# A macaron block on one core: the planner of the issue order also tries 180 random shifts of urgency

## The chip, the cores and the metric

The kernel runs on one core of one Trainium2 chip. The metric is the device time in microseconds (us) of one execution, as the median of some runs. The engines are PE (TensorE, matmuls and transpositions), DVE (VectorE), ACT (ScalarE), POOL (GpSimd) and SP (SyncE, which here only issues DMAs). Each engine works through its own list of instructions in order; an instruction that waits for a semaphore holds up all that stand behind it on that engine.

## The reference

The input is 8 sequences of 1024 tokens with 256 features, in float32. Three residual parts follow each other:

```python
x = x + 0.5 * ffn(layernorm(x))
x = x + mamba(layernorm(x))
x = x + 0.5 * ffn(layernorm(x))
```

- `ffn`: gate and up matrices of 704 x 256, `silu(gate) * up`, and a down matrix of 256 x 704. Ahead of each of the three matmuls the activations, and once the weights, are rounded in blocks of 16 values to a grid of eight magnitudes (FP4) and scaled back.
- `mamba`: a normalisation, a projection to 2 x 512 channels x and z, a causal convolution of four taps over x and `silu`, a projection to a step size `delta` (softplus) and to B and C of 16 states, and the selective scan

```python
h = exp(delta * A) * h + delta * B * u     # over time, for 512 channels x 16 states
y = sum over the states of h * C  +  u * D
```

then `y * silu(z)` and a projection back to 256 features.

## The kernel before, in words

The tokens are cut into 16 chunks of 512, two to a sequence (`SPLIT`). For every chunk there are generators for the first feed-forward part (`stage_f1`), what precedes the scan (`stage_m1`), the z branch (`stage_z`), the scan (`scan`), and the output projection with the second feed-forward part (`stage_out`). The list `work` at the end of `macaron` interleaves them: the first feed-forward part of a chunk is emitted some chunks ahead of its scan and the second one behind it. So at any time the scan of one chunk shares the engines with feed-forward work of others.

The scan of a chunk runs over 16 states, k. For each state (`scan_step`): ACT scales the transposed `delta * u` by B (s_bu, L793, four tiles); then for each of four groups of 128 channels ACT computes the decay (s_da, L797), PE transposes s_bu into a PSUM bank (s_pb, L800, four transpositions; two banks, "psb", take turns), and DVE runs the recurrence over 512 steps (s_h, L802). If the sequence goes on, ACT keeps the last column (s_carry, L828). POOL multiplies the four groups by C, two at a time (`times_c`, L810), and then issues a DMA that adds the product to a sum in DRAM (accd, L835; the second state of a chunk stores plainly through SP instead). Four buffers hold s_h.

The feed-forward part of 128 tokens: PE makes half of gate (f_pg) and of up (f_pu, both L559), ACT takes a tanh (L562), DVE multiplies twice (L563, L564) into f_h. The rounding (`quant`) is a chain over three engines: DVE takes the blocks' maxima (q_mx, L459), POOL the scale (q_sc, L460), DVE its reciprocal (q_rc, L461), POOL multiplies (L462), ACT squares into PSUM (q_q, L466), DVE makes two passes that round (L467, L468), POOL multiplies by the scale (L469). The same chain runs over the normalised input, f_xn. Then PE transposes f_h (f_pa, f_pb), ACT copies (f_ht, L572, L576), PE multiplies by the down matrix (f_po, L579), and DVE adds to the residual x4 (L580).

The order of issue is not that of emission. When all is emitted, `set_order` (L338) builds a `Graph` of all instructions: `price` gives each one a cost by engine, kind and size; `LAG` what a semaphore between two engines takes (105 ns from POOL to POOL); buffers that are used again are edges as well. `Graph.plan` lays out a schedule on this model: it takes the engine that can start first and, of its instructions that are ready, the one with the smallest `prio`, with a little look-ahead (`LOOK`, `WAIT`). It models POOL and DVE holding a shared port, PE's start from cold, and one server for all DMAs. Run with `back=True`, it lays out the schedule from the end.

`set_order` makes a first plan from the order of emission and the longest path behind each instruction (L342), and then `PASSES` = 7 rounds: a plan from the end gives each instruction its latest start, and these starts are the priorities of the next plan from the front (L343 to L345). Of the eight plans, the one with the least total is taken (L347), and its order on each engine is written into the program as dependencies without semaphores. The instructions themselves, their buffers and their semaphores follow from the emitted program and from this order.

Of the kernel before, what the change touches and what calls it, by code (L numbers as in the profile page):

```python
# [3 lines left out]

# [75 lines left out]

WEIGHT = 0.2
LOOK = 600
WAIT = 30
PASSES = 7
TICK = 10240 / 3
PORT = 200
SLACK = 20000
# [82 lines left out]
class Graph:  # L172
# [85 lines left out]
    def plan(self, prio, back=False):  # L258
# [18 lines left out]
        while len(order) < self.n:  # L277
# [40 lines left out]
            if not back and e == ET.PE:  # L318
                if passed[t // TICK - 1] < WARM:
                    more = hold  # L320
                passed[(t + hold + more) // TICK] += cols
                free[e] += more
# [15 lines left out]
def set_order(tc, tags, nbuf):  # L338
    insts = [i for i in tc.nc.cur_bb.bb.instructions if type(i).__name__ != "BassTilePoolBoundary"]
    g = Graph(insts, tags, nbuf)  # L340
    path = g.paths()
    found = [g.plan([x - WEIGHT * path[x] for x in range(g.n)])]  # L342
    for _ in range(PASSES):  # L343
        total, _, start = g.plan([-s - c[0] for s, c in zip(found[-1][2], g.cost)], back=True)
        found.append(g.plan([total - s - c[0] for s, c in zip(start, g.cost)]))  # L345
    prev = {}
    for x in min(found, key=lambda f: f[0])[1]:  # L347
        e = g.eng[x]
        if e in prev:
            tc.add_manual_dep(insts[x], insts[prev[e]].name, mybir.DependencyInfo(  # L350
                mybir.DependencyClass.NoSync, mybir.DependencyReason.DATA), reason="issue order")
        prev[e] = x
# [3 lines left out]
def macaron(ctx: ExitStack, tc: tile.TileContext, x_in, norm_w, norm_b, in_w, conv_w,  # L356
# [505 lines left out]
    for _, _, gen, kind[0] in sorted(work, key=lambda w: w[:2]):  # L862
        next(gen, None)
    set_order(tc, tags, nbuf)


# [26 lines left out]
```

## Time and profile before

| what | value |
|---|---|
| median of three runs | 2534.21 us (2523.82 to 2535.66) |
| the profiled execution: time | 2536.37 us |
| the profiled execution: span from first to last instruction | 2534.4 us |
| PE busy | 2344.9 us (93%), 10980 matmuls |
| DVE busy | 2184.4 us (86%), 3082 instructions |
| ACT busy | 2146.9 us (85%), 3952 instructions |
| POOL busy | 2177.2 us (86%), 1556 instructions |
| mean granted clock of PE | 0.985 |
| products h * C on POOL (L810) | 512, 1281.8 us, mean 2596 ns |
| accumulating DMAs from POOL (L835) | 238, 1024 KB each, 9.7 us to landing |

The profile is of one execution. Busy times are unions of the instructions' spans; an engine's idle time is what is left of the span. A float32 matmul or transposition is one instruction in the program; the profile can show a matmul as two. A wait names the instruction that stood still, and the one whose semaphore came last. The chain of waits goes back from the last instruction to what released each piece of it. A "product" below is an L810, a "scan step" an L802.

### The profile page before, as it was taken

How to read it: one execution, taken by the hardware profiler on the slowest of the kernel's cores; microseconds unless marked ns; L12 is line 12 of the kernel's file. 1: busy time of each engine (PE TensorE's matmuls, PEld its weight loads, DVE VectorE, ACT ScalarE, POOL GpSimd, SP SyncE). 2: the span in 40 equal slices, each digit the busy share in tenths (PEclk: the TensorE clock that was granted, in tenths of full speed). 3: DMA queues.
4: the chain of work that ended last, by engine and by line, in shares of the span. 5: the costliest groups of instructions: out<-in, count | busy, mean ns of one | idle time of the engine just before them, and what ended most of it. 6: DMA issues, size and time to landing. Idle time of an engine off the chain costs nothing.

```text
span 2534.4 us, 33625 instructions
## 1 busy us (share of the span) xinstructions
PE 2344.9 (93%) x10980; PEld 1591.6 (63%) x10980; DVE 2184.4 (86%) x3082; ACT 2146.9 (85%) x3952; POOL 2177.2 (86%) x1556
## 2 busy tenths in 40 slices
PE   5989898999999999999999999999999999888876
PEld 3555565766666666666666666666666666655544
DVE  7568797998989899898989899898989989878885
ACT  4489787998989988999888989898989988999842
POOL 4359798899989999899998999899997999899952
PEclk9989999999999999999999999999999999999998
DMA  3049779699888988789897998889896988999950
GB/s 90 9 117 207 194 163 223 163 186 238 166 197 195 218 202 189 205 171 239 176 219 173 201 221 176 211 173 221 195 202 181 189 225 175 216 235 211 232 127 17
DMA packets 113647, 465.57 MB, mean 184 GB/s; under 512 B 14592, under 2 KB 32896, under 8 KB 76864
## 3 DMA queue, kind: packets, MB, share of 16 engines
q0 software_dynamic: 36576, 266.35, 56.3%
q1 hardware_dynamic: 76896, 197.08, 24.2%
q8 instruction: 86, 1.41, 0.2%
q14 instruction: 89, 0.73, 0.1%
HBM read 146.19 MB, written 317.19 MB: 183 GB/s over the span
## 4 chain that ended last, share of the span: by engine, by line
POOL 36%; PE 27%; issue 11%; DVE 9%; ACT 9%; DMA 8%; POOLq 0%; SPq 0%; DVEq 0%; ACTq 0%
POOL s_h L810 20%; PE f_pg L559 4%; PE f_pu L559 4%; PE f_po L579 4%; PE s_pb L800 4%; POOL accd L835 4%; DVE s_h L802 4%; DMA accd<-s_h 3%; PE m_pc L682 3%; POOL f_h L462 3%; POOL f_h L469 3%; ACT s_bu L793 2%; ACT s_da L797 2%; POOL f_xn L469 2%; POOL o_y L771 2%
## 5 line engine op out<-in xcount | busy, mean ns | idle before, releaser
L810 POOL TENSOR_TENSOR s_h<-s_h,s_cbc 128x1024 f32<-128x1024 f32 x512 | 1281.8, 2596 | 51.7 <-ACT s_carry L828 27.0
L797 ACT ACTIVATE s_da<-m_delta,an 128x512 f32<-128x512 f32 x1024 | 714.5, 715 | 44.5 <-DVE s_h L802 42.8
L793 ACT ACTIVATE s_bu<-m_duT,m_bc 128x512 f32<-128x512 f32 x1024 | 693.4, 715 | 15.6 <-PE s_pb L800 14.1
L800 PEld LDWEIGHTS s_pb<-ident,s_bu 128*128 128x128 f32 x4096 | 498.0, 142 | 330.2 <-issue 123.4
L800 PE MATMUL s_pb<-ident,s_bu 128*128 128x128 f32 x4096 | 639.2, 277 | 50.9 <-DVE s_h L802 47.4
L802 DVE TENSOR_TENSOR_SCAN s_h<-s_da,s_carry,s_pb 128x512 f32<-128x512 f32 x512 | 636.5, 1265 | 16.5 <-PE s_pb L800 13.3
L802 DVE TENSOR_TENSOR_SCAN s_h<-s_da,s_pb 128x512 f32<-128x512 f32 x512 | 604.4, 1206 | 35.0 <-PE s_pb L800 21.1
L579 PE MATMUL f_po<-wdn,f_ht 128*128 128x256 f32 x1536 | 393.1, 387 | 11.5 <-ACT f_ht L576 6.8
L559 PE MATMUL f_pg<-wg,f_xt 128*128 128x352 f32 x1024 | 370.5, 473 | 13.7 <-ACT f_xt L549 6.2
L559 PE MATMUL f_pu<-wu,f_xt 128*128 128x352 f32 x1024 | 365.6, 468 | 14.1 <-DVE f_h L563 8.4
L579 PEld LDWEIGHTS f_po<-wdn,f_ht 128*128 128x128 f32 x1536 | 276.1, 192 | 73.3 <-ACT f_ht L576 17.0
L835 POOL DMA_DIRECT2D accd<-s_h x238 | 230.7, 969 | 31.8 <-POOL s_h L810 24.1
L559 PEld LDWEIGHTS f_pu<-wu,f_xt 128*128 128x128 f32 x1024 | 182.6, 193 | 115.7 <-issue 34.5
L682 PE MATMUL m_pc<-m_xp,cdg 128*128 128x512 f32 x512 | 252.7, 595 | 2.4 <-ACT m_car L679 2.4
L469 POOL TENSOR_TENSOR f_h<-f_h,q_sc 128x704 f32<-128x704 f32 x128 | 206.5, 1616 | 54.9 <-DVE f_h L468 50.5
L559 PEld LDWEIGHTS f_pg<-wg,f_xt 128*128 128x128 f32 x1024 | 180.3, 195 | 93.4 <-issue 15.1
L462 POOL TENSOR_TENSOR f_h<-f_h,q_rc 128x704 f32<-128x704 f32 x120 | 184.9, 1541 | 22.7 <-DVE q_rc L461 21.9
L563 DVE SCALAR_TENSOR_TENSOR f_h<-f_h,f_pg 128x352 f32<-128x352 f32 x256 | 128.7, 506 | 86.4 <-ACT f_h L562 85.5
L460 POOL TENSOR_SCALAR q_sc<-q_mx 128x44 f32<-128x44 f32 (+2 forms) x198 | 98.0, 497 | 88.5 <-DVE q_mx L459 83.8
L564 DVE TENSOR_TENSOR f_h<-f_h,f_pu 128x352 f32<-128x352 f32 x256 | 129.5, 507 | 41.6 <-PE f_pu L559 39.9
L562 ACT ACTIVATE f_h<-f_pg 128x352 f32<-128x352 f32 x256 | 115.6, 456 | 48.1 <-PE f_pg L559 46.6
L776 PE MATMUL o_po<-outw,o_y 128*128 128x256 f32 x512 | 129.3, 387 | 5.5 <-POOL o_y L771 2.9
(110 smaller groups left out, 3299.6 us busy)
## 6 DMA issues: line engine op xcount, KB each, us to landing
accd<-s_h POOLq DMA_DIRECT2D x238, 1024.0 KB, 9.7
s_cbc<-cd SPq DMA_DIRECT2D x128, 512.0 KB, 5.6
accd<-m_ud SPq DMA_DIRECT2D x64, 256.0 KB, 9.3
accd<-s_h SPq DMA_DIRECT2D x16, 1024.0 KB, 6.8
szd<-m_tz SPq DMA_DIRECT2D x64, 256.0 KB, 6.8
o_y<-accd SPq DMA_DIRECT2D x16, 1024.0 KB, 9.9
o_y<-accd POOLq DMA_DIRECT2D x16, 1024.0 KB, 9.1
o_sz<-szd SPq DMA_DIRECT2D x30, 512.0 KB, 5.1
```

What stands on the lines that cost most here:

```text
L462: mul0.tensor_tensor(vb, vb, rc.unsqueeze(2).to_broadcast([P, g, BLK]), ALU.mult)
L469: mul1.tensor_tensor(vb, vb, sc.unsqueeze(2).to_broadcast([P, g, BLK]), ALU.mult)
L559: nc.tensor.matmul(dst, xt[:, c, :], w[:, c, hf * FH : (hf + 1) * FH], start=(c == 0), stop=(c == 1))
L564: nc.vector.tensor_tensor(hh, hh, pu, ALU.mult)
L579: nc.tensor.matmul(po, ht[:, k, :], wdn[:, k, :], start=(k == 0), stop=(k == NF - 1))
L682: nc.tensor.matmul(pc, cdg[:, dc, k, :], xp[:, k : k + n], start=(k == 0), stop=(k == KC - 1))
L793: nc.scalar.activation(b, duT[s][t], AF.Copy, scale=bcol[s][:, t, k : k + 1])
L797: nc.scalar.activation(da, delta[s][dc], AF.Exp, scale=an[:, dc, k : k + 1])
L800: nc.tensor.transpose(pb[:, t * P : (t + 1) * P], bu[t][:, dc * P : (dc + 1) * P], ident)
L802: nc.vector.tensor_tensor_scan(h[:, dc, :], da, pb, init, ALU.mult, ALU.add)
L810: eng_c.tensor_tensor(hv, hv, cbc.unsqueeze(1).to_broadcast([P, cm, n]), ALU.mult)
L835: nc.gpsimd.dma_start(accd[s][j, :, :, :n], h, accum_op=ALU.add)
```

## The change

In `set_order` the loop of passes keeps the best plan of those that the seven passes made and its priorities (`prio`) rather than a list. The first plan of all counts only until the first pass. Then the instructions are grouped by the kind of tile that they write (its name without the number) and by engine; groups of fewer than 16 are left out. With a generator of fixed seed, 180 trials follow. Each takes one to three groups, draws for each a shift from a normal distribution with a spread of 1, 4 or 12 us, adds it to the priorities of all instructions of that group, and plans anew. A trial whose total is below the best is kept, and the next trial starts from its priorities. The order of the best plan is written into the program as before. All that stands behind it is as it was, 25 lines further down.

```diff
+import random
...
+TRIALS = 180
+SHIFT = (1e3, 4e3, 12e3)
...
-    found = [g.plan([x - WEIGHT * path[x] for x in range(g.n)])]
+    best = last = g.plan([x - WEIGHT * path[x] for x in range(g.n)])
+    prio = None
     for _ in range(PASSES):
-        total, _, start = g.plan([-s - c[0] for s, c in zip(found[-1][2], g.cost)], back=True)
-        found.append(g.plan([total - s - c[0] for s, c in zip(start, g.cost)]))
+        total, _, start = g.plan([-s - c[0] for s, c in zip(last[2], g.cost)], back=True)
+        late = [total - s - c[0] for s, c in zip(start, g.cost)]
+        last = g.plan(late)
+        if prio is None or last[0] < best[0]:
+            best, prio = last, late
+    groups = defaultdict(list)
+    for x, i in enumerate(insts):
+        for a in i.outs:
+            if hasattr(a, "bass_ap"):
+                groups[a.bass_ap.tensor.name.rsplit("_", 1)[0], g.eng[x]].append(x)
+    groups = [u for u in groups.values() if len(u) >= 16]
+    rng = random.Random(4)
+    for _ in range(TRIALS):
+        late = list(prio)
+        for u in rng.sample(groups, rng.choice((1, 2, 3))):
+            d = rng.gauss(0.0, rng.choice(SHIFT))
+            for x in u:
+                late[x] += d
+        f = g.plan(late)
+        if f[0] < best[0]:
+            best, prio = f, late
     prev = {}
-    for x in min(found, key=lambda f: f[0])[1]:
+    for x in best[1]:
```

## The prediction

> **What bounds the kernel now.** I read the stretches first: busy time from the start to the first scan step (157 us), from there to the last scan step (2443 us), and behind it. Columns: sum of the stretch, then busy us (and instructions) of PE, its weight loads, DVE, ACT and POOL, the granted clock, DMA share and GB/s.
>
> ```profile
> 0.00:157.00 157.00, 123.15 (x437) 77.30 (x438) 93.26 (x171) 79.17 (x166) 58.05 (x79) 0.96 0.20 61
> 157.00:2443.00 2286.00, 2157.97 (x10304) 1471.44 (x10301) 2037.34 (x2823) 2048.05 (x3746) 2099.38 (x1455) 0.99 0.88 198
> 2443.00:2534.00 91.00, 63.77 (x242) 42.83 (x242) 53.76 (x89) 19.71 (x41) 19.82 (x23) 0.90 0.11 31
> ```
>
> The middle is nine tenths of the time. No engine is full in it: PE is idle for 128 us of 2286, POOL for 187, ACT for 238, DVE for 249. Four engines at 89 to 94% that hand short pieces to each other: the end is set by who waits for whom. The chain that ended last says the same; no engine has half of it:
>
> ```profile
> POOL 36%; PE 27%; issue 11%; DVE 9%; ACT 9%; DMA 8%; POOLq 0%; SPq 0%; DVEq 0%; ACTq 0%
> ```
>
> Then the waits of the middle stretch: engine and line, what it waited for, total us, times, longest. The longest three each of POOL, ACT and DVE, and the one of PE that matters:
>
> ```profile
> DVE f_h L563 <- ACT f_h L562: 63.7, 52, 7.4
> PE s_pb L800 <- DVE s_h L802: 47.4, 77, 2.5
> ACT s_da L797 <- DVE s_h L802: 42.8, 69, 1.9
> DVE s_h L802 <- PE s_pb L800: 34.4, 57, 2.6
> DVE q_rc L461 <- POOL q_sc L460: 33.3, 31, 5.0
> ...
> POOL q_sc L460 <- DVE q_mx L459: 28.9, 20, 8.9
> ...
> ACT q_q L466 <- POOL f_h L462: 27.8, 36, 2.4
> POOL s_h L810 <- ACT s_carry L828: 27.0, 18, 5.0
> ...
> POOL accd L835 <- POOL s_h L810: 24.1, 80, 0.4
> ...
> ACT m_delta L709 <- PE m_pd L708: 18.2, 11, 3.4
> ```
>
> The reader is to see many small waits, none of which is a bottleneck by itself. Leaving out waits for DMA and an engine's waits for itself, the named waits between engines add up to 128.7 us on POOL, 219.7 on DVE and 180.9 on ACT in this stretch.
>
> **What the change does to the order.** The same instructions are issued; only their order on each engine differs. I set the built order of the changed kernel against that of before, instruction by instruction. The first 125 instructions of ACT are the same, the first scan step stands at place 285 on PE in both and at 174 and 175 on DVE; behind the last product of the scan POOL has 27.6 and 23.8 us of work left, DVE behind the last scan step 52.0 and 50.5. So **start and end get nothing**: PE is the busiest engine in both, and the 4 us on POOL lie beside its matmuls. In the middle much moves, but not far: of the neighbouring pairs PE keeps 72%, POOL 40%, ACT 38%, DVE 32%; a scan step moves back by 1.4 places on DVE, the quantising passes over f_h and f_xn (L467, L468) forward by 1.3 and 1.8. The feed-forward part became a little more urgent, the scan a little less.
>
> **The terms.** A wait inside a round trip can be counted from an order: A on engine X releases B on Y, B releases C on X. The work between A and C on X, at the mean durations of the trace, is the cover; if it is short, C waits. I sorted the round trips of before by cover, took the mean idle time ahead of C in each class from the trace, and counted the classes again in the new order.
>
> 1. PE's scan banks. Two PSUM banks take the transposed s_pb, so the block after next (L800) needs the scan step (L802) done. Of 1022 trips, cover under 0.65 us: 35 before, 29 after, at 0.56 us of PE idle each; 0.65 to 1.35: 77 and 58 at 0.24; 1.35 to 2: 318 and 334 at 0.03; over 2: 592 and 601 at nearly nothing. 6 x 0.56 + 19 x 0.24 - 16 x 0.03 = **7.4 us less**, of 50.4 in all: 15%.
> 2. The quantising trips on DVE (L459 to L461 by POOL, L461 to L467 by POOL and ACT), f_h and f_xn. Mean cover falls, 5.23 to 4.54 and 6.19 to 5.68 us for the second trip. By classes: -0.7 and +2.9 for f_h, +2.6 and +7.7 for f_xn, **12.5 us more** on DVE. The same trips as POOL sees them (L460 to L462, L462 to L469): +2.9, +1.0, +1.4, -2.1, **3.2 us more**.
> 3. POOL's accumulating DMA (L835). Where it stands right behind the product whose result it sends, POOL idles 0.33 us ahead of it; behind anything else, 0.03 us (82 and 156 in before). The new order has 116 of the first kind: 34 x 0.29 = **9.9 us more** on POOL. Behind it in POOL's queue stand the next products and quantising steps, and the scan waits for them.
> 4. PE changes its kind of work 3196 times and not 2984. A transposition starts 144 ns ahead of a following f_po matmul and 131 ns ahead of its own kind: 13 ns x 212 = 2.8 us more on PE, if nothing hides it.
> 5. The products on POOL (L810) fall into classes: 152 of 512 last under 2.45 us, 282 last 2.45 to 2.76, 78 more. Which DVE work lies beside each is redrawn. If a twentieth, 26, change class either way, that is 26 x 0.27 = 7 us less or more; I take nothing.
> 6. All other waits between engines can't be counted from one engine's order, and these are what the trials aim at. Bounds: nothing, and the 128 us that PE is idle in the middle, the smallest idle sum. I take the share of term 1, 15% (0.147 unrounded), the only one with a count: it is a wait of the same kind and size as the others. That is my choice, and the weakest step.
>
> On term 5 the Trainium skill speaks against this change: "SBUF — State Buffer", section "SBUF: two separate sides", says that DVE and GpSimd take their shared port pair as an exclusive lock for a whole instruction, whichever starts first, and the other fully blocks. The two classes of the product's duration in this trace agree with that, but show no blocker by name. By the rule the duration of a product hangs on a few hundred ns of phase, which no plan made beforehand can hold over 2286 us; the plan's gain at that port would then be lost, and the sum would stand at its upper part. The sum here doesn't use it.
>
> **The sum.** Busy time in the middle does not change, so each engine's account is its idle time. POOL: -0.147 x 128.7 + 9.9 + 3.2 = -5.8. DVE: -0.147 x 219.7 + 12.5 = -19.8. ACT: -0.147 x 180.9 = -26.6. They must end at one figure; I take their mean, **-17.4 us** (PE's busy time has modelled ends, so its account is a rival below). The profiled execution took 2536.37 us, span 2534.4, 0.1% above the median of 2534.21 of the three runs, so nothing is converted: 2536.4 - 17.4 = **2519 us**, 0.6% below the median.
>
> **Rivals.** (a) PE's account is right: only terms 1 and 4 reach the end, -7.4 + 2.8 = -4.6, **2532 us**. For: PE has least idle time, and the chain is on it for 27%. Against: its waits in the profile are short, and POOL has more of the chain. (b) Slower: POOL's DMA issue. The waits that the trials take away come back at other places (shorter covers in term 2 point there), and what stays is POOL's line with products and issues back to back: from the end of a product to the start of what follows its DMA take 1.04 us when the issue stands directly behind it, 0.62 otherwise; 34 x 0.42 = 14.3 us more, **2551 us**. It decides once term 6 gives POOL less than 13 us. For: POOL has 36% of the chain, and the wait is on POOL itself, where no better timing elsewhere helps. Against: the wait is known to the planner, though at less than its measured size (0.105 us in its table). (c) The gain is twice my share: POOL -24.7, DVE -52.1, ACT -53.2, mean -43, **2493 us**. (d) That the trials keep nothing is excluded: the order differs.
>
> **Chances.** Forecast 0.42, (c) 0.06, (a) 0.32, (b) 0.20. About 0.5%, 13 us, is what a measurement of this kernel tells from no change: faster by more is the forecast and (c), 0.48; within it (a), 0.32; slower (b), 0.20. The forecast lies near the border, which is why (a) has so much. The range goes from (c) to (b), 2493 to 2551, and takes in the 7 us of term 5.
>
> **What would show it.** Busy sums equal within a per cent on DVE and ACT. Right: PE's wait for L802 in the middle down from 47.4 to about 40; the sums between engines down by a tenth or more on ACT and DVE; POOL's wait of L835 for L810 up from 24.1 to about 34 with some 114 occurrences; first scan step at 157 us and 91 us behind the last one, as now. Wrong: POOL's busy time over the products moved by more than 10 us (term 5), a new wait for DMA landings (the slots of s_h return sooner or later), or a start or end that moved by more than 5 us.

## The result, and the profile after

| | median us | runs | ratio, 95% |
|---|---|---|---|
| before | 2533.2 | 2523.82 to 2535.66 (4) | 1 |
| after | 2555.07 | 2552.52 to 2556.48 (4) | 1.0083, 1.0061 to 1.0105 |

The changed kernel is slower by 0.8%, where 0.6% faster was forecast; the time lies above the range. The profiled execution took 2554.48 us, with a span of 2552.7, 18.3 us more than before. Line numbers are now those of the changed kernel, 25 higher. First the stretches, cut in the same way (start, from the first scan step to the last, behind it), with the same columns:

```profile
0.00:155.00 155.00, 121.35 (x447) 75.72 (x448) 95.79 (x174) 80.44 (x169) 58.58 (x81) 0.98 0.21 64
155.00:2469.00 2314.00, 2170.71 (x10303) 1472.92 (x10301) 2040.74 (x2827) 2045.31 (x3745) 2103.16 (x1455) 0.98 0.87 196
2469.00:2553.00 84.00, 60.52 (x234) 42.10 (x234) 49.28 (x83) 19.09 (x39) 17.71 (x21) 0.89 0.07 22
```

The busy sums of DVE, ACT and POOL in the middle are those of before within 4 us; PE's is 13 us larger, at a granted clock of 0.98 and not 0.99. Measured exactly from the first scan step to the last, the middle grew from 2288.0 to 2314.2 us, and start and end gave back 4 us each. For DVE, ACT and POOL that is 24 to 28 us more of idle time, for PE 14. The waits of the middle (engine and line, what it waited for, total us, times, longest), the largest without PE's weight loads, and those that moved:

```profile
ACT s_da L822 <- DVE s_h L827: 60.8, 79, 2.2
PE s_pb L825 <- DVE s_h L827: 53.3, 82, 2.7
DVE f_h L588 <- ACT f_h L587: 50.2, 41, 7.1
DVE q_rc L486 <- POOL q_sc L485: 43.8, 44, 5.4
POOL accd L860 <- POOL s_h L835: 35.1, 116, 1.0
...
ACT m_duT L754 <- PE m_dt L752: 33.3, 21, 6.8
...
DVE bn_st L548 <- DMA x4c<-x1d: 21.9, 6, 5.7
DVE f_h L492 <- ACT q_q L491: 20.4, 27, 2.0
...
ACT m_tz L768 <- DMA accd<-m_ud: 14.5, 3, 8.0
```

The chain of waits is spread as before (POOL 33%, PE 27%, DVE 11%) and names no culprit. In the waits two lines for DMAs are of a new size. The load of x4c (L667) fetches the residual ahead of the Mamba part of a chunk; DVE waits 21.9 us for it in 6 places, against 4.5 in 4 before. ACT waits 14.5 us for a buffer that the store of m_ud (L745) reads, against 3.3.

Summed anew over every group of both traces, from the first scan step to the last, us before and after:

| waits of | for other engines | for DMAs | for itself |
|---|---|---|---|
| PE | 123.3, 137.5 | 0, 0 | 0, 0 |
| POOL | 131.8, 133.2 | 14.1, 20.1 | 27.2, 38.8 |
| DVE | 230.9, 236.9 | 4.9, 22.3 | 0, 0 |
| ACT | 210.3, 235.6 | 17.3, 23.5 | 0.2, 0 |

On DVE 17 of the 24 us more are for DMAs. On POOL the waits for other engines stayed as they were, and its own issue and the DMAs added to them. On ACT the growth is for other engines: for the scan step (s_da, 42.8 to 60.8) and for PE's transpositions (m_duT, 16.6 to 33.3). So in no engine did the waits for others fall.

What such a place looks like, at a border between two chunks near 1000 us; first the two stretches in the columns of above:

```profile
985.00:1000.00 15.00, 15.00 (x74) 10.16 (x73) 12.71 (x14) 13.13 (x21) 14.40 (x10) 1.00 1.01 253
1000.00:1015.00 15.00, 8.07 (x20) 4.10 (x19) 6.09 (x15) 6.44 (x10) 8.44 (x6) 0.70 1.03 257
```

Then what SP issued there in the kernel after (start, duration, line, transfer), and two of the instructions that stood waiting, on DVE and on PE; the bracket has the idle time ahead of an instruction and what ended it:

```profile
986.24 0.32 SPq L656 DMA_DIRECT2D x1d<-x4a  x1
988.50 0.32 SPq L745 DMA_DIRECT2D accd<-m_ud  x1
988.92 0.94 SPq L844 DMA_DIRECT2D s_cbc<-cd  x1
992.73 0.32 SPq L667 DMA_DIRECT2D x4c<-x1d  x1
```

```profile
1004.72 0.75 DVE L548 BATCH_NORM_STATS2 bn_st<-x4c 128x6 f32<-128x256 f32 x2 [3.77 <-DMA x4c<-x1d]
```

```profile
1006.41 2.71 PE L584 MATMUL f_pu<-wu,f_xt 128*128 128x352 f32 x4 [3.65 <-DVE f_h L588]
```

The reader is to see that the DMA share (the column ahead of GB/s) is 1.0 for 30 us: all 16 DMA engines are full. The load of x4c, issued at 992.73, lands 12 us later. DVE stands, then PE for 3.65 us, and the granted clock of that stretch is 0.70. The same border before: three stretches, SP's issues, and DVE's first read of x4c:

```profile
985.00:1000.00 15.00, 15.00 (x80) 10.88 (x78) 14.84 (x20) 13.65 (x24) 14.65 (x11) 1.00 1.01 203
1000.00:1015.00 15.00, 15.00 (x73) 10.22 (x72) 13.12 (x15) 11.53 (x20) 14.70 (x10) 1.00 1.03 258
1015.00:1030.00 15.00, 14.49 (x63) 9.04 (x62) 10.93 (x20) 13.85 (x23) 12.28 (x11) 1.00 1.00 292
```

```profile
1006.46 0.32 SPq L631 DMA_DIRECT2D x1d<-x4a  x1
1007.52 0.58 SPq L720 DMA_DIRECT2D accd<-m_ud  x1
1014.72 0.32 SPq L642 DMA_DIRECT2D x4c<-x1d  x1
1015.79 0.32 SPq L819 DMA_DIRECT2D s_cbc<-cd  x1
```

```profile
1025.33 0.43 DVE L523 BATCH_NORM_STATS2 bn_st<-x4c 128x6 f32<-128x256 f32 x1 [0.72 <-DMA x4c<-x1d]
```

Before, too, the DMA share is 1.0, for 45 us, and the load, issued at 1014.72, takes 10.6 us. But DVE has other work until then: it waits 0.72 us for x4c and not 3.77, and PE hardly pauses. Over all 15 loads the time from issue to landing is much the same in both kernels, 8.5 us in the median before and 8.7 after (the longest 12.2 and 13.6), while DVE's wait for them is five times as long. So full DMA engines and slow landings are no news of the order after. At this border it has less other work at hand until the load lands.

The lists of SP differ as well. At this border the broadcast of C (s_cbc) is issued ahead of the load after, and behind it before. Between a chunk's store of x1d and its load of x4c it stands at 9 of the 15 borders after, and at 4 before.

The two traces also differ in their course. After is 17 us ahead where chunk 4 (of 16) begins its scan, 725.7 against 742.8 us, and 19 us behind at chunk 13, 2079.8 against 2061.1.

### The profile page after: what moved, and what is told of

Same layout as the page of the kernel before. It is cut to its first block, busy times and chain, and to the rows that moved or that the text cites. A ratio compares the mean times of both kernels' runs of the same rounds, so it can differ in the third digit from the quotient of the medians.

```text
span 2552.7 us, 33598 instructions
## 1 busy us (share of the span) xinstructions
PE 2352.6 (92%) x10980; PEld 1590.8 (62%) x10980; DVE 2185.8 (86%) x3082; ACT 2144.8 (84%) x3952; POOL 2179.5 (85%) x1556
## 3 DMA queue, kind: packets, MB, share of 16 engines
q0 software_dynamic: 36576, 266.35, 56.1%
q1 hardware_dynamic: 76896, 197.08, 24.4%
## 4 chain that ended last, share of the span: by engine, by line
POOL 33%; PE 27%; DVE 11%; issue 10%; ACT 10%; DMA 8%; POOLq 0%; SPq 0%; DVEq 0%; ACTq 0%
POOL s_h L835 18%; DVE s_h L827 6%; PE f_pg L584 5%; PE f_po L604 4%; PE f_pu L584 4%; PE s_pb L825 4%; POOL accd L860 3%; ACT s_da L822 3%; POOL f_h L487 3%; ACT s_bu L818 3%; POOL f_h L494 2%; DMA accd<-m_ud 2%; PE m_pc L707 2%; DMA x4c<-x1d 2%; PE o_po L801 1%
## 5 line engine op out<-in xcount | busy, mean ns | idle before, releaser
L835 POOL TENSOR_TENSOR s_h<-s_h,s_cbc 128x1024 f32<-128x1024 f32 x512 | 1288.7, 2593 | 50.1 <-ACT s_carry L853 34.9
L822 ACT ACTIVATE s_da<-m_delta,an 128x512 f32<-128x512 f32 x1024 | 717.0, 716 | 63.8 <-DVE s_h L827 60.8
L825 PE MATMUL s_pb<-ident,s_bu 128*128 128x128 f32 x4096 | 646.4, 278 | 56.1 <-DVE s_h L827 53.3
L604 PE MATMUL f_po<-wdn,f_ht 128*128 128x256 f32 x1536 | 401.3, 385 | 7.1 <-ACT f_ht L597 3.3
L584 PE MATMUL f_pu<-wu,f_xt 128*128 128x352 f32 x1024 | 376.8, 476 | 23.3 <-DVE f_h L588 19.3
L584 PE MATMUL f_pg<-wg,f_xt 128*128 128x352 f32 x1024 | 375.7, 476 | 16.5 <-DVE f_h L588 9.8
L604 PEld LDWEIGHTS f_po<-wdn,f_ht 128*128 128x128 f32 x1536 | 270.4, 192 | 71.6 <-issue 16.8
L860 POOL DMA_DIRECT2D accd<-s_h x238 | 223.4, 939 | 47.5 <-POOL s_h L835 35.1
L494 POOL TENSOR_TENSOR f_h<-f_h,q_sc 128x704 f32<-128x704 f32 x128 | 200.4, 1570 | 68.7 <-DVE f_h L493 66.7
L487 POOL TENSOR_TENSOR f_h<-f_h,q_rc 128x704 f32<-128x704 f32 x120 | 184.4, 1538 | 25.1 <-DVE q_rc L486 22.5
L491 ACT ACTIVATE q_q<-f_h 128x704 f32<-128x704 f32 x128 | 97.1, 759 | 49.6 <-POOL f_h L487 36.1
```

The costliest lines, as they stand in the source:

```text
L487: mul0.tensor_tensor(vb, vb, rc.unsqueeze(2).to_broadcast([P, g, BLK]), ALU.mult)
L494: mul1.tensor_tensor(vb, vb, sc.unsqueeze(2).to_broadcast([P, g, BLK]), ALU.mult)
L584: nc.tensor.matmul(dst, xt[:, c, :], w[:, c, hf * FH : (hf + 1) * FH], start=(c == 0), stop=(c == 1))
L604: nc.tensor.matmul(po, ht[:, k, :], wdn[:, k, :], start=(k == 0), stop=(k == NF - 1))
L822: nc.scalar.activation(da, delta[s][dc], AF.Exp, scale=an[:, dc, k : k + 1])
L825: nc.tensor.transpose(pb[:, t * P : (t + 1) * P], bu[t][:, dc * P : (dc + 1) * P], ident)
```

## The experiments

Four theories stood against each other at first: late landings and the buffers they hold, of x4c and m_ud, cost the time (A); POOL's DMA issue behind its own product, rival (b) of the prediction, does (B); the many short waits of engines on each other do, whatever the DMAs do (C); the model's error is larger than its gain, so that a plan's rank says nothing of the chip (D). Formed on the way: the load of the DMA engines eats the gain (F); the order's early part is good and its later part bad (G); the order of SP's list, s_cbc ahead of x4c, does it (H). Every kernel was compared with its own runs of the kernel before, whose medians were 2531.4 to 2536.5 us. An "a" at the front of a name is the order after, a "b" the order before; the others have orders of their own.

### The landings: other sources and more buffers

a_x4c loads the residual from the input instead of from the store ahead of it; the planner is told the old dependency, so that the order stays. b_both and a_both have that and t2k (m_tz's and m_ud's buffers) with one buffer more.

```diff
-            nc.sync.dma_start(x4[:, :nt], x1d[s][:, :nt])
+            nc.sync.dma_start(x4[:, :nt], tok(x_in, s))
```

> The order of the changed kernel, instruction for instruction; only x4c (L642 in the numbering of before) is loaded from the input instead of from x1d, so that the load no longer waits for the store of x1d to land. The planner is still told of the old dependency, so the plan and all orders are the same. Left out: the first feed-forward part does not reach what the scan part reads. Theory A (landings: the new order puts users of DMAs earlier than they land; DVE stands still for x4c for 21.9 us in the changed kernel against 4.5 before): this wait falls under 5 us and the time by 12 to 20 us, to 2535 to 2543. Theory B (POOL's accumulating DMA issues stand right behind their products, 116 times against 82): nothing of it is touched, time within 5 us of 2555. Theory C (the scan step was made less urgent by 4 us, so ACT and PE wait for it): within 5 us of 2555.

Measured: 1.0128 (1.0111 to 1.0145), slower still. The wait for x4c went from 21.9 to 30.4 us: the load now stood waiting for its buffer, which an x1d store still had to read. It is also another load: from the input the same bytes come in four times the packets (82656 against 76896 on SP's queue, 384 more for each of the 15 loads).

a_t2k has only the fourth t2k buffer; for the room, the second half of the input projection's z weights is left out (the first half is read in its place):

```diff
-            xc = sb.tile([P, T], F32, tag="t2k", bufs=BUFS["t2k"], name="m_xc")[:, :n]
+            xc = sb.tile([P, T], F32, tag="t2k", bufs=BUFS["t2k"] + 1, name="m_xc")[:, :n]
```

> The order of the changed kernel, instruction for instruction; the tiles of the tag t2k (m_xc, m_ud, m_tz) get four buffers instead of three, so that m_tz need not wait until the DMA of an earlier m_ud has been read out (14.5 us of ACT's waits in the changed kernel, 3.3 before, and 15.3 against 3.5 us of DVE's for m_tz itself). To make room the second half of the z weights is left out (its matmuls read the first half's weights); the planner counts as before. Theory A (landings): these two waits fall under 5 us each and the time by 6 to 12 us, to 2543 to 2549. Theories B (POOL's DMA issues) and C (late scan steps): within 4 us of 2555.

> Both edits on the order of the changed kernel: x4c from the input, four buffers for t2k (left out: the first feed-forward part for the scan part, half of the z weights). Theory A (landings): waits for DMAs fall from 31 us on DVE and 26 on ACT to under 12 each; the time goes to 2525 to 2538, level with the kernel before. Theory B: 2555 less 5 at most, since its 11 us on POOL stay. Theory C: 2548 or more, since the waits for the scan step stay at 60.8 us on ACT and 53.3 on PE.

> The same two edits on the order of the kernel before (same parts left out). It shows how much these waits cost there: its waits for DMAs are 15 us on DVE and 20 on ACT. Theory A: 3 to 8 us less than 2533, so 2525 to 2530, and with both edits the two orders lie within 10 us of each other. Theories B and C: the distance of 20 us between the two orders remains with both edits.

Measured: a_t2k 1.004 (1.0026 to 1.0055), with ACT's wait for m_ud at 0; a_both 1.0078 (1.0049 to 1.0106); b_both 1.0001 (0.9984 to 1.0018). So the missing buffer is worth about 11 us to the order after. What it is worth to the order before isn't shown: b_both holds the other source too, which by itself cost the order after some 11 us.

a_x4t gives x4 and t2k a buffer more each; a_all and b_all add the other source.

```diff
-        x4 = sb.tile([P, NT, DM], F32, tag="x4", bufs=BUFS["x4"], name="x4a")
+        x4 = sb.tile([P, NT, DM], F32, tag="x4", bufs=BUFS["x4"] + 1, name="x4a")
```

> The order of the changed kernel, instruction for instruction, with four x4 buffers instead of three and four t2k buffers instead of three; the planner still counts three of each. To make room, in_proj keeps 256 of its 1024 columns and the other column groups read these again (the other three quarters of these weights are left out). The load of x4c then waits neither for the release of a buffer nor m_tz for the transfer of m_ud. Loading x4c from the input had changed nothing (DVE's wait for it 30.4 us, it had been 21.9), so it was not the store of its own x1d that held it. Theory A (the plan lets DMAs of SP land too early): wait for x4c under 8 us, m_tz's under 3, time 2528 to 2540. If the wait for x4c stays, it is the transfer itself behind other queues. Theory B (POOL's DMA issues) and C (late scan steps): 2543 as with t2k alone, or more.

> The order of the changed kernel with all three edits at once: x4c from the input, four x4 buffers, four t2k buffers (left out as told for the single edits; in_proj keeps 256 of its columns). The single edits on x4c had each left the other reason to wait: with the input as source the load still waited for its buffer, until the store of an earlier x4a had landed, and with the fourth buffer it still waited for x1d to land. Theory A: now DVE's wait for x4c goes from 22 us to under 3, m_tz's stays away, the PE pauses over 2.5 us between the first and the last scan step go from 8 to 3 or fewer, and the time to 2525 to 2534. If the wait goes and the time stays at 2538 to 2545, these waits were a third of the loss and the rest is elsewhere.

> The order of the kernel before with the same three edits: the control. Theory A: 2522 to 2530, within 8 us of the changed order with these edits. Theory D (a plan comes out at random): the distance stays 12 us or more.

Measured: a_x4t 1.0043 (1.0026 to 1.006), the wait for x4c still 25.1 us; a_all 1.0065 (1.0044 to 1.0085); b_all 1.0001 (0.9989 to 1.0014). The fourth x4 buffer thus adds nothing to the fourth t2k buffer. In a_all nothing holds the load's issue any more, and it is issued earlier. The tile's view of a_all, who waited for what, and the time from issue to landing:

```profile
  DMA x4c<-_attn_hidden_states_dram: 31.9, 7
...
DMA to landing us min/median/max: 4.7/15.3/21.0
```

In the kernel after, and then in the kernel before:

```profile
  DMA x4c<-x1d: 21.9, 6
...
DMA to landing us min/median/max: 3.9/8.7/13.6
```

```profile
  DMA x4c<-x1d: 4.5, 4
...
DMA to landing us min/median/max: 3.8/8.5/12.2
```

One load, issued at 844.1 us instead of 847.6, landed at 861.2 instead of 861.0; the next, issued at 991.4 instead of 992.7, landed at 1012.4 instead of 1004.7. So the loads of a_all won nothing by their earlier issue, but they are the ones with four times the packets, and what an earlier issue of the same load would bring isn't shown. Theory A holds for the buffer of m_ud, worth about half of the loss; for x4c it stays open.

### The planner told of later landings, and other seeds

land0 and land180 add 1500 ns to the landing of SP's DMAs in the model; land0 has no trials.

```diff
-d = 0 if not full else hold + late + (1560 if self.dma[y] else LAG[self.eng[y], self.eng[x]])
+d = 0 if not full else hold + late + ((1560 + 1500 * (self.eng[y] == ET.SP)) if self.dma[y] else LAG[self.eng[y], self.eng[x]])
```

> The changed kernel with no trials (0), but its Graph counts 1.5 us more from any DMA that SP issues to those who wait for it (the trace has 8.7 us median from issue to landing for x4c; the planner has 3.5 us plus its queue). This is the kernel before but for that constant; its control. Theory A: 2515 to 2530, a little less than 2533, because waits for DMAs fall from 15 us on DVE and 20 on ACT. Theory D (a plan is a coin toss of about 10 us whatever the planner counts): 2523 to 2555.

> The changed kernel with its 180 trials, and 1.5 us more from a DMA of SP to those who wait for it. Theory A (the trials spent a slack that the plan thought free, because its DMAs land too early): with the landing priced, what the trials find stays: 2495 to 2518, faster than land0 by 5 us or more. Theory D (the trials fit the order to the planner's times, and on the chip any such plan comes out at random): 2530 to 2560, not below land0.

Measured: land0 1.0084 (1.006 to 1.0108), land180 1.0074 (1.0058 to 1.0091). A constant is no cure. Why it doesn't even help stays open. And land0, which has no trials, is as slow as after: a plan of this planner can come out 21 us above that of before with no trial in it.

s1 and s2 have another seed:

```diff
-    rng = random.Random(4)
+    rng = random.Random(1)
```

> The changed kernel with the generator's seed 1 instead of 4, nothing else: another walk of 180 trials on the same planner. Theory A: slower than before as well, since the walk runs against the same early landings: 2540 to 2570, with waits for DMAs on DVE and ACT above 45 us together. Theory D: anywhere from 2520 to 2565. If it is faster than 2520, the loss belongs to the one walk of seed 4.

> The changed kernel with seed 2; a third walk. Its planner's own total falls by 9 us against the best of the passes; that of seed 1 fell by 27 and of seed 4 by 23. Seed 1 took 2533 us, seed 4 2555. Theory D: 2525 to 2560, in no order with the planner's total. If the planner's total told the chip's time at this scale, seed 2 would lie between before and seed 1, at 2533.

Measured: s1 1.0007 (0.9995 to 1.0019), s2 1.0031 (1.0014 to 1.0048). The plans' own totals (worked out by the planner, no times of a chip) are 23, 27 and 9 us below that of before for seeds 4, 1 and 2; the chip gave +22, +2 (by its ratio) and +8. None of the three gains came through. The plan promised much where the chip gave nothing, but the sign isn't random: all three lie above what was promised, by 45, 29 and 17 us. Three seeds and land0 don't exclude D: the kernel before may simply be a plan that came out well.

### POOL's issue

a_swap exchanges, wherever POOL's DMA issue stands right behind the product that it sends, the issue with the next instruction, if that one doesn't depend on it.

```diff
+        if g.dma[x] and any(q == p and full for q, full, _ in g.before[x]) and all(q != x for q, _, _ in g.before[y]):
+            pool[k], pool[k + 1] = y, x
```

> The changed kernel, all orders as they are but POOL's: an accumulating DMA issue that stands right behind the product it sends changes places with the instruction behind it, if that does not need it. The 116 such places become 4 or fewer. Theory B (POOL idles 0.3 us ahead of each, and the new order has 34 more of them): the wait of L835 for L810 falls from 35 us to under 3 and the time by 8 to 15 us, to 2540 to 2547. If POOL's issue is off the path, or the later issue holds back a buffer: within 4 us of 2555, or above.

Measured: 1.0056 (1.0037 to 1.0075). POOL's wait for its own product went from 35.1 to 0.6 us, its waits for DMAs rose from 20 to 42. Of the 34.5 us about 7 reached the end (1.0083 to 1.0056), and as the two intervals overlap it may be less. B is at most a minor part.

### The DMA engines lightened

a_noacc and b_noacc store the products plainly. Left out is the sum over the states; the bytes of the product, the count of DMAs and both issue orders stay.

```diff
-                    nc.gpsimd.dma_start(accd[s][j, :, :, :n], h, accum_op=ALU.add)
+                    nc.gpsimd.dma_start(accd[s][j, :, :, :n], h)
```

> The order of the changed kernel; the 238 DMAs from POOL store the products without adding to what is there (left out: the sum over the states; fewer bytes for the DMA engines to read). All orders are the same. Theory F (crowding of the DMA engines at the chunk borders: there the new order issues s_cbc and an accumulating store some 4 us ahead of x4c, and lands x4c in 12 to 14 us rather than 4 to 7): x4c lands in 4 to 8 us, DVE's wait for it falls under 6 us, and the time by 15 to 35 us, to 2520 to 2540, level with or below the kernel before treated the same way. If landings don't change or the time stays within 6 us of 2550, F falls.

> The order of the kernel before with plain stores from POOL, the control. Theory F: 5 to 15 us less than 2533 and above or level with a_noacc, since without crowding the planner's 23 us would come through. Theory D (a plan falls out at random on the chip): it stays 12 us or more below a_noacc.

Measured, on one chip: a_noacc 2464.22 us, 0.9712 (0.969 to 0.9734); b_noacc 2481.34 us, 0.9778 (0.9755 to 0.9801). **The order after is now the faster one, by 17 us, of 23 that its plan promised.** The DMA queue of POOL (packets, MB, the time of the packets as a share of 16 engines' span), after and a_noacc:

```profile
q0 software_dynamic: 36576, 266.35, 56.1%
```

```profile
q0 software_dynamic: 36576, 266.35, 28.3%
```

For the same bytes, its packets take half as long. The waits for x4c are gone (median landing 6.9 us, at most 8.4). The slices of the span, DMA share in tenths, after and a_noacc:

```profile
DMA  3049789899888989798888988788897898999960
```

```profile
DMA  3035546557464656557465564646565474766540
```

How near the chip comes to the plan says the same. From the last scan step's planned to its measured start it is 67 us before and 104 us after, but 11 us in a_noacc and 10 in b_noacc. By these figures the plan promised 14 us up to that step, and with plain stores the chip gave 13.5 (2390.1 to 2376.6 us). The waits for other engines fell there too, from b_noacc to a_noacc: POOL 149.9 to 124.4 us, DVE 186.9 to 171.8, ACT 179.0 to 171.8. With plain stores the model's times fit, and what it calls shorter is shorter.

What makes it fit isn't parted by this pair, for plain stores also lighten POOL, in both orders alike (busy in the middle 2103 to 2032 us and 2101 to 2032). The groups of POOL, after and then a_noacc: busy us, mean ns of one, idle time ahead:

```profile
L835 POOL TENSOR_TENSOR s_h<-s_h,s_cbc 128x1024 f32<-128x1024 f32 x512 | 1288.7, 2593 | 50.1 <-ACT s_carry L853 34.9
L860 POOL DMA_DIRECT2D accd<-s_h x238 | 223.4, 939 | 47.5 <-POOL s_h L835 35.1
```

```profile
L835 POOL TENSOR_TENSOR s_h<-s_h,s_cbc 128x1024 f32<-128x1024 f32 x512 | 1205.8, 2366 | 70.7 <-ACT s_carry L853 42.9 <-DVE s_h L827 22.9
L860 POOL DMA_DIRECT2D accd<-s_h x238 | 145.1, 610 | 43.8 <-POOL s_h L835 33.5 <-issue 5.9 <-POOL m_xp L700 2.8
```

The second of these also says that POOL's wait for its own product, 33.5 us, is as long as ever in the faster of the two kernels: B doesn't make the order after slow.

The planner's own prices point at POOL. `price` has 2.32 us for a product and 0.64 us for POOL's issue of a DMA. That is close to what a_noacc shows (2.37 and 0.61); the kernel after takes 2.59 and 0.94. For the time of the DMA engines it has 5.67 us for each MB that POOL sends, which is what an accumulating one was measured at (5.6 us, worked out at the end), and too much for a plain one (2.7). In the two plans the load of x4c lands 7.9 us (before) and 9.3 us (after) behind its issue in the median, worked out by the planner; measured it was 8.5 and 8.7. So with accumulating DMAs the model prices POOL's product a tenth and its issue a third too low, and the DMA engines about right. No run changed POOL's prices or its speed alone, so this rival of theory F stands untested.

### Which part of the order, and SP's list alone

hyb_ab has the order after for all that its plan starts before 716 us, and the order of before behind; hyb_ba the reverse.

```diff
+    early = {x for x in range(g.n) if best[2][x] < 716e3}
+    order = [x for x in best[1] if x in early] + [x for x in passes[1] if x not in early]
```

> The two orders put together in time: all instructions that the changed plan starts before its 716 us (chunk 4) in the changed order, the rest in the order of before. Theory G (each stretch of a plan is good or bad by itself; the changed order gained 17 us up to chunk 4 and lost 36 from there to chunk 13): the early gain stays, 2512 to 2525. If the gain is paid back whatever the order behind it is, because the engines' lead over each other at the seam is lost: 2530 to 2545.

> The reverse: the order of before up to its 718 us (chunk 4), the changed order from there. Theory G: the loss behind chunk 4 without the gain ahead of it, 2560 to 2580. If the loss came from the early part (engines that got out of step there), 2530 to 2545.

Measured: hyb_ab 2523.58 us, 0.995 (0.9932 to 0.9969); hyb_ba 1.0124 (1.0103 to 1.0146). hyb_ab leaves nothing out and beats both kernels. Starts of the first scan step of a chunk and of the last step, from the traces, in us:

| | chunk 4 | chunk 13 | last scan step | span |
|---|---|---|---|---|
| before | 742.8 | 2061.1 | 2446.9 | 2534.4 |
| after | 725.7 | 2079.8 | 2469.4 | 2552.7 |
| hyb_ab | 732.6 | 2047.5 | 2439.2 | 2526.7 |
| hyb_ba | 739.2 | 2094.9 | 2483.3 | 2567.6 |
| b_noacc | 719.3 | 2009.6 | 2390.1 | 2478.7 |
| a_noacc | 714.9 | 1999.3 | 2376.6 | 2461.5 |

From chunk 4 to chunk 13, the order after takes 1354 us in after and 1356 in hyb_ba, the order of before 1318 and 1315. The loss lies in the repeated part of the order, 150 us a chunk against 146, and doesn't depend on the way in. With plain stores it is 1284 against 1290. The early part of the order after is a gain even with accumulating DMAs: from the first scan step to chunk 4 it takes 570.6 us against 583.9 before, at a DMA share of 0.87 against 0.85. So a high mean DMA share alone does not make this order lose.

b_sp has the orders of before on the four engines, and only SP's list of after. a_x4first is after, with s_cbc behind the load of x4c where it stood up to four places ahead of it.

```diff
+    rest = iter([x for x in best[1] if g.eng[x] == ET.SP])
+    order = [next(rest) if g.eng[x] == ET.SP else x for x in passes]
```

```diff
+        if name[k].startswith("x4c") and j is not None and not any(n.startswith("x1d") for n in name[j:k]):
+            sp.insert(j, sp.pop(k))
```

> The order of the kernel before on PE, DVE, ACT and POOL, and SP's list from the changed kernel. Theory H (the order of SP's DMAs at the chunk borders makes the loss): x4c lands in 9 to 14 us where s_cbc stands ahead of it, and the time rises to 2543 to 2556. If the crowding comes from when the other engines hand over their results, it stays within 5 us of 2533.

> The changed kernel; in SP's list alone, an s_cbc that stands up to four places ahead of a load of x4c, with no store of x1d between them, goes behind it. Theory H: x4c lands in 5 to 9 us, DVE's wait for it falls from 22 to under 8 us, and the time to 2535 to 2545, unless the later s_cbc makes POOL wait as much. If the crowding is not SP's order: within 5 us of 2551.

Measured: b_sp 1.0092 (1.0069 to 1.0114), a_x4first 1.004 (1.0022 to 1.0058). SP's list alone makes the kernel before as slow as after, though by another wait: x4c costs only 5.6 us there, but POOL waits for the load of the gate z, 4.2 us before. Among POOL's waits of b_sp (lines of that kernel):

```profile
POOL o_y L799 <- DMA o_sz<-szd: 23.2, 10, 9.6
```

And the load of x4c in a_x4first:

```profile
  DMA x4c<-x1d: 9.9, 4
...
DMA to landing us min/median/max: 3.7/6.5/10.8
```

Moving a few DMAs on SP gives back about 11 us of the 21: roughly half, with POOL's work as it was (a product 2596 ns in the mean). The loss in b_sp shows that SP's list matters; as it comes by another wait and from two lists that were not planned together, it doesn't show how after loses. After with the whole SP list of before can't be run: the lists of the engines then wait for each other in a circle. Fewer buffers elsewhere weren't tried.

## Why the prediction was wrong, point by point

- **Term 6, 15% of all other waits, and the waits for DMA put at nothing beside it: this step failed.** It took 18.9 us off POOL's waits for other engines, 32.3 off DVE's and 26.6 off ACT's. Measured, they became 1, 6 and 25 us longer, and the waits for DMAs 6, 17 and 6 us longer; that is the growth of the idle time. The trials' gain was one in the planner's model. It comes through with plain stores (17 us of the promised 23 in a_noacc against b_noacc, the waits for other engines down by 17%, 8% and 4% on POOL, DVE and ACT), and not with the accumulating DMAs of the kernel that runs. The prediction left out waits for DMA without a reason, though 0.88 stood in the DMA column of its stretches. No rival had a price for them; only the list of signs named them.
- **The sums that term 6 worked on** (128.7, 219.7 and 180.9 us) hold only the longest groups of each engine. Complete, in the same stretch, they are 139.5, 230.8 and 210.6; and the 8.9 us at POOL's q_sc ended before the first scan step. This changes the sum by a few us and not its sign.
- **Term 1, PE's scan banks, -7.4 us: wrong sign.** 47.4 became 53.3. The covers were counted in the built order and stand, but a class's mean wait holds only if the scan step starts when it can. That a late DVE spoils this is our reading; it wasn't tested.
- **Term 2, quantising trips, +12.5 on DVE: right direction, under-sized.** q_rc 33.3 to 43.8, f_h behind q_q 9.6 to 20.4, f_xn 8.4 to 5.8: +18.7. On POOL, in the order of the term, +0.5, +12.9, +2.2 and -7.7: +7.9, with +3.2 forecast; the second place has most of the error, and the fourth takes a part of it back by luck.
- **Term 3, POOL's issue: right.** 24.1 to 35.1 us, in 116 places; +11.0 with +9.9 forecast. Rival (b) gave the right side and, with 2551 us, nearly the time from this cost. That is luck: a_swap takes the whole wait away, and some 7 us of the 21 go with it.
- **Term 4, kinds of work on PE, 2.8 us:** the 144 and 131 ns are means with idle time in them. In the trace of before the median from the start of a transposition to the next instruction is 109 ns in both cases, so the trace shows no cost of a change of kind. PE's added busy time in the middle (13 us) can't be split by kind, as it has modelled ends and a lower clock in it.
- **Term 5, the products: right within its bound of 7,** 1281.8 to 1288.7 us, in part by luck. The class from 2.45 to 2.76 us gained 47 and not 26, and the classes below and above it lost 17 and 30.
- **The rule on the port (the Trainium skill, "SBUF — State Buffer", section "SBUF: two separate sides"), weighed for term 5:** DVE alone doesn't make the two classes of product in this kernel. Between 2.45 and 2.76 us lay 282 of 512 before and 329 after; in a_noacc and b_noacc 501 to 504 of 512 last less than 2.45 us, beside the same busy time of DVE. The measurement decides: the longer class goes with the accumulating DMAs. No run here showed the lock.
- **Start and end get nothing:** both became 4 us shorter, 158.9 to 155.1 and 87.4 to 83.3 us, which the kinds of work there didn't tell.
- **No clock in the sum.** PE's pauses over 2.5 us in the middle rose from 2 to 8, and the mean granted clock of the whole span fell from 0.985 to 0.979. PE's busy time there grew by 12 us, from 2158.8 to 2171.0; times the granted clock of each 100 us it did not grow (2140 and 2135), so the 12 us are about what the lower clock made of the same work. The one dip looked at lies at a pause (0.70 at the border above). How much of the 18 us the clock makes by itself wasn't parted.

Shown: the loss is in the middle, in the repeated part; the order after is the better one with plain stores and the worse one with accumulating DMAs; moving s_cbc behind x4c gives about half of the loss back, and so does the fourth t2k buffer; the waits between engines did not fall. Not shown: whether accumulating DMAs turn the sign through the time of the DMA engines or through POOL, which they slow beyond the planner's prices; whether the two halves add up; and whether the kernel before is a plan that came out well among many. The cause stays open to that extent.

## What to carry to other kernels

A search that minimises a planner's total can gain in the model and lose on the chip. Compare the planner's prices with the profile of the kernel that will run, under its own load, before the search; here they fitted a kernel without the accumulating DMAs. Lightening what the model doesn't hold and comparing both orders again is a quick test of whether an order is bad or only meets something unpriced; count what else that edit makes faster. Before a full resource is blamed for a loss, look at the same place in the faster kernel: it can be as full there. And a load that comes late can be helped by putting less urgent transfers behind it.

## What the runs showed of the hardware that was not expected

- The packets of a DMA of 1 MB that accumulates in DRAM hold the 16 DMA engines about twice as long as those of a plain one. Worked out from the queues' shares, spans and the 254 DMAs of that size on q0 (266.35 MB): 0.561 x 2552.7 / 254 = 5.6 us against 0.283 x 2461.5 / 254 = 2.7 us; 238 of the 254 are the accumulating ones.
- With accumulating DMAs, POOL's own work is slower than with plain ones: a product 2593 against 2366 ns, the issue of a DMA 939 against 610 ns, in the same order.
- From issue to landing a load of 512 KB (x4c) took 3.8 to 12.2 us before and 3.9 to 13.6 after; with plain stores it took 3.6 to 11.0 and 3.7 to 8.4.
- In 15 us at a border in which PE was busy for 8.07 us, the granted clock was 0.70; at the same border before, with PE busy for 14.5 us or more of each 15, it was 1.00.
